# Expert slots from both ends: half of each expert's blocks gathered without the routing of the last four sequences

## The chip, the cores and the metric

The kernel runs on one core of a Trainium2 chip. The metric is the device time of one execution in microseconds (us); the median of several executions is compared. Of the core's engines, PE is TensorE's matmuls (PEld its weight loads), DVE is VectorE, ACT ScalarE, POOL GpSimd and SP SyncE. Every engine works through its own instructions in order. SP and POOL issue the DMAs of this case; POOL issues the indirect ones, which gather or scatter rows by an index held in SBUF.

## The reference

Thirty-two sequences of 256 tokens with 256 features each (8192 tokens) go through two layers. The first layer is a modulated linear map, a gated attention, an adapter, and a block of self-attention and a mixture of experts. The second is a linear attention with adapters and a feed-forward network whose two matrices are products of ten butterfly stages each. What matters here is the mixture of experts, cut short:

```python
C = 0.25 * T                                    # 2048 slots for each of 8 experts
logits = x @ wr;  probs = softmax(logits)
top1 = argmax(probs);  top2 = argmax(logits without top1)
loc1 = cumsum(m1, axis=0) - 1                   # m1, m2: one-hot of the choices
loc2 = cumsum(m2, axis=0) - 1 + m1.sum(0)       # second choices behind all first ones
m1 = m1 * (loc1 < C);  m2 = m2 * (loc2 < C)     # what doesn't fit is dropped
t1, t2 = probs of the kept choices, divided by their sum
# each expert: relu(x w1 + b1) w2 + b2 over its slots; y times t1 or t2 is added to the token
```

Which slot of its expert a token gets makes no difference to the result, as long as the same choices are dropped.

## The kernel before, in words

The program has two phases. The first makes the first layer up to the routing logits `L_all`, sequence after sequence. The second has the experts, the making of the butterfly matrices, and the second layer ("answers"). Between them stands a branch on a value read from memory (L1440), by which the first phase can be computed again in another form; it isn't taken here. No instruction of the second phase starts before it.

Within a phase, parts of the program are Python generators, which a planner (`side_by_side`, L100) runs side by side when the program is built. `yield PE, 0.5` gives the engine and the cost of the next piece, `yield "join", part` waits for another part, `get` and `back` take and return a tile of a ring, and `Turns` limit how many parts are in a section. The planner simulates the engines with these costs, takes what can start first (by order in the list at L2465 where several can), and so fixes the order of instructions on each engine. Rings: "mm" (the 8 PSUM banks), "sh" (small work tiles in SBUF, among them gathered rows `xg`, products `ysb` and butterfly products `bft`), and "big" (weights, hidden activations, butterfly weights `bfw`).

Routing goes by 64 token tiles of 128 tokens (`NT`). The last 8 (`LATE`), which are the last four sequences, are routed in the second phase, since their logits come last; the 56 before ("early") while the first phase still runs (`routed_early`, L664). The steps are the same for both:

- `choices_of` (L526) finds both choices on DVE (L548 to L556).
- `places_of` (L559) counts choices by tile and expert on PE (`cnt`, L569) and adds counts of tiles before and a triangular product (`loc`, L582 and L584) to the place of every choice in its expert (`nths`). All first choices of an expert are numbered through and so are the second choices.
- `tokens_of` (L597) turns places into slots and inverts the map: one-hot products on PE (`tps`, L626; one-hots from DVE and ACT) give the token in each slot. First choices get slots from the front of an expert (0, 1, ...), second choices from the back (2047, 2046, ...).

In `routing` (L1503), the second phase's part, the two halves are added (`both`, L1514), `late` tells which slots hold a second choice, and `tok` (L1520) is the table of tokens by slot. `ends` (L1527) makes the masks `late` and `used` from the totals; `gates` (L1568) makes the weights, transposes them on PE (L1612) and writes them to `gbuf` in memory (L1618); `slots` makes index tables `grow` and `row`.

An expert has 2048 slots in 4 blocks of 512. `expert_block` (L1675) waits for `routed`, gathers the rows of a block in 4 gathers on POOL (L1686), transposes them on PE (L1700) into `ehT`, and multiplies by w1 (L1740) and w2 (L1757). `slot_gates` (L1627) gathers the weights of the block's slots (`gslot`, L1633), `ysb` is multiplied by them (L1772), and `add_to_tokens` (L1638) adds each 128 rows to the tokens by an indirect scatter (L1643), one at a time. `load_expert` (L1659) loads w1, w2 and b2 of an expert over SP; expert 1's loads and the butterfly's are held behind the first block's gathers by a small memset on POOL (`behind_gathers`, L1653). `butterflies` runs ten stages (L1799 to L1805, three sections each) on DVE; PE takes the first half's result at L1834.

Of the kernel before, what the change touches and what calls it, by code (L numbers as in the profile page):

```python
# [218 lines left out]
def network(ctx: ExitStack, tc: tile.TileContext, a: dict, out: bass.AP):  # L219
# [303 lines left out]
    cntb = cst.tile([P, 2, NSB], BF, name="cntb")  # L523
    early = cst.tile([P, 2, 2 * NHI], F, name="early")

# [34 lines left out]
    def places_of(a, b):  # L560

        W = b - a
        n0, n1 = a // SLAB, -(-b // SLAB)
        wide = [(min(b, (n + 1) * SLAB) - n * SLAB) * NE for n in range(n1)]
        cps = yield from get("mm", "cnt", [P, 2, NSB])
        yield PE, 0.07 * 2 * (n1 - n0)
        for k in range(2):
            for n in range(n0, n1):
                nc.tensor.matmul(  # L569
                    cps[: wide[n], k, n : n + 1], mbs[:, k, n * P : n * P + wide[n]], oneb, start=True, stop=True  # L570
                )
        for n in range(n0, n1):
            yield DVE, 0.15
            nc.vector.tensor_copy(cntb[: wide[n], :, n], cps[: wide[n], :, n])
        yield back("mm")
        step = 2 if 2 * W * NE <= 512 else 1
        for k0 in range(0, 2, step):
            shape = [P, step, W * NE]
            loc = yield from get("mm", "loc", shape)
            yield PE, (1 + n1) * step * (0.05 + W * 0.0065)  # L580
            for i in range(step):
                nc.tensor.matmul(loc[:, i, :], utb, mbs[:, k0 + i, a * NE : b * NE], start=True, stop=False)  # L582
                for n in range(n1):
                    nc.tensor.matmul(  # L584
                        loc[:, i, :], cntb[: wide[n], k0 + i, n : n + 1].to_broadcast([wide[n], P]),
                        before[: wide[n], n, a * NE : b * NE], start=False, stop=(n == n1 - 1),
                    )
            e3 = yield from get("sh", "e3", shape)
            yield DVE, 0.1 + step * W * 0.0095
            nc.vector.tensor_tensor(e3, loc, mbs[:, k0 : k0 + step, a * NE : b * NE], ALU.mult)  # L590
            yield back("mm")
            yield DVE, 0.1 + step * W * 0.0095
            nc.vector.tensor_reduce(
                nths[:, k0 : k0 + step, a:b], e3.rearrange("p k (t e) -> p k t e", e=NE), AX.X, ALU.add
            )
            yield back("sh")

    def tokens_of(a, b, wide, into):
# [10 lines left out]
        nc.vector.tensor_scalar(f[:, 0], nth, float(CAP), float(2 * NSL), ALU.is_gt, ALU.mult)  # L609
        for k, (op, at) in enumerate(((ALU.add, NE * CAP - 1), (ALU.subtract, (NE + 1) * CAP))):  # L610
            nc.vector.scalar_tensor_tensor(f[:, 1, k], firsts[:, k, a:b], -float(CAP), nth[:, k], ALU.mult, op)
            nc.vector.scalar_tensor_tensor(i[:, 0, k], f[:, 1, k], float(at), f[:, 0, k], ALU.add, ALU.add)
# [5 lines left out]
        yield back("sh")  # L618
        tps = yield from get("mm", "tps", [P, 2, 2 * NHI])
        into.append(tps)  # L620
        last = None

        def product(ol, oh, k, t, w):
            yield PE, 0.135 * w
            for i in range(w):
                nc.tensor.matmul(  # L626
                    tps[:, k, :], ol[:, i // 2, :, i % 2], oh[:, i // 2, :, :, i % 2].rearrange("p a h -> p (a h)"),
                    start=(t + i == 0), stop=(t + i == W - 1),
                )
            yield back("sh")  # L630
            yield back(wide)

        def by_place(ol, oh, o1, k, t, w, before):
            yield ACT, 0.15 + 0.125 * w
            nc.scalar.activation(oh[:, :, 1, :, :], o1, AF.Copy, scale=prow)
            yield back("sh")
            if before is not None:
                yield "join", before
            yield from product(ol, oh, k, t, w)
# [24 lines left out]
    def routed_early(sequences):  # L664
# [6 lines left out]
        yield from tokens_of(0, NT - LATE, "kk", got)  # L671
        yield DVE, 0.8
        nc.vector.tensor_copy(early, got[0])
        yield back("mm")

# [824 lines left out]
    used = column_h("used")  # L1500
    cc = wD.tile([P, 2, NE], F, name="cc")

    def routing():  # L1503
# [5 lines left out]
        yield from tokens_of(NT - LATE, NT, "big", got)  # L1509
        both = yield from get("sh", "both", [P, 2, 2, NHI])  # L1510
        to = wD.tile([P, 2, NHI], F, name="to")
        yield "join", counted
        yield DVE, 0.75
        nc.vector.tensor_add(both.rearrange("p k a h -> p k (a h)"), got[0], early)  # L1514
        yield back("mm")
        yield DVE2, 1.0
        nc.vector.tensor_tensor(to, both[:, 1], late.unsqueeze(1).to_broadcast([P, 2, NHI]), ALU.mult)
        nc.vector.tensor_add(to, to, both[:, 0])
        yield DVE, 0.3
        nc.vector.scalar_tensor_tensor(tok, to[:, 0], float(P), to[:, 1], ALU.mult, ALU.add)  # L1520
        yield back("sh")
        rest.append(Part(gates()))
# [4 lines left out]
    def ends():  # L1527

        ps = yield from get("mm", "mm", [P, 2, NE])
        yield PE, 0.5  # L1530
        for k in range(2):
            for n in range(NSB):
                w = min(SLAB, NT - n * SLAB) * NE
                nc.tensor.matmul(
                    ps[:, k, :], cntb[:w, k, n : n + 1].to_broadcast([w, P]), e8b[:w],
                    start=(n == 0), stop=(n == NSB - 1),
                )
        yield DVE, 0.15
        nc.vector.tensor_copy(cc, ps)
        yield back("mm")  # L1540
        from_ = wD.tile([P, NE], F, name="from_")
        E3 = [P, NE, CAP // P]
        yield DVE, 1.0
        nc.vector.tensor_scalar(from_, cc[:, 1, :], -1.0, float(CAP), ALU.mult, ALU.add)
        for o, v in ((late, cc[:, 0, :]), (used, from_)):
            nc.vector.tensor_tensor(
                o.rearrange("p (e h) -> p e h", e=NE), place.unsqueeze(1).to_broadcast(E3),
                v.unsqueeze(2).to_broadcast(E3), ALU.is_ge,
            )
        nc.vector.scalar_tensor_tensor(used, late, 0.0, used, ALU.is_equal, ALU.max)  # L1550

# [16 lines left out]
    def gates():  # L1568

        pr = yield from get("sh", "pr", W3)  # L1570
        e3 = yield from get("sh", "e3", W3)
        sm_, den = column("sm_"), column("den")
        yield DVE2, 0.7
        nc.vector.tensor_tensor(pr, L_all, bc(tops[:, 0, :]), ALU.subtract)
# [8 lines left out]
        for k in range(2):  # L1583
            m = mbs[:, k, :].rearrange("p (t e) -> p t e", e=NE)
            s_ = nths[:, k, :]
            if k == 1:

                s_ = column("s1")
                yield DVE2, 0.7
                nc.vector.tensor_tensor(e3, m, cc[:, 0, :].unsqueeze(1).to_broadcast(W3), ALU.mult)  # L1590
                yield DVE, 0.9
                nc.vector.tensor_reduce(s_, e3, AX.X, ALU.add)
                nc.vector.tensor_add(s_, s_, nths[:, k, :])
            g = column(f"g{k}")
# [31 lines left out]

    def slot_gates(j0):  # L1627
        for p in rest:
            yield "join", p
# [20 lines left out]

    gathered, turned_first = Part(_ for _ in ()), Part(_ for _ in ())

# [6 lines left out]
    def load_expert(e, w):  # L1659
# [6 lines left out]
        yield SP, 0.1  # L1666
        nc.sync.dma_start(w["w1"], a["w1"][e].rearrange("(c p) f -> p c f", p=P))
        yield SP, 0.1
        nc.sync.dma_start(w["w2"], a["w2"][e].rearrange("(f p) d -> p f d", p=P))
        yield SP, 0.1  # L1670
        nc.sync.dma_start(w["b2"], a["b2"][e : e + 1, :].to_broadcast([P, D]))
        yield DMA, 10.5
        yield None, 2.0

    def expert_block(e, blk, w, loaded, routed):  # L1675
        yield lanes_b
        yield "join", routed
        s0 = e * CAP + blk * CBLK
# [5 lines left out]
        for t in range(QT_):  # L1684
            j = s0 // P + t
            nc.gpsimd.indirect_dma_start(  # L1686
                xg[t], None, h2buf[:, :], bass.IndirectOffsetOnAxis(ap=tok[:, j : j + 1], axis=0)
            )
# [24 lines left out]
        yield weights  # L1713
        yield "join", loaded
        yield hid_turn
# [14 lines left out]
        for q0 in range(0, QT_, wide):  # L1730
# [17 lines left out]
            for p in rs:  # L1748
                yield "join", p
            each = 1 if last else 2  # L1750
            for t0 in range(q0, q0 + wide, each):
                n = min(each, QT_ - t0)
# [710 lines left out]
    with tc.manual_schedule():  # L2463
        side_by_side(
            [routed, loads[0], blocks[0], loads[1], matrices, *blocks[1:], weights_part, *loads[2:], table_part, *first_parts, square_part, norm_part, rows_part]  # L2465
            + [Part(answer_out(b, first_parts[-10] if b < 2 else norm_part, [norm_part])) for b in range(B)],
# [127 lines left out]
```

## Time and profile before

| | us |
|---|---|
| median of 3 runs | 3633.08 |
| lowest, highest | 3620.55, 3637.11 |
| profiled execution | 3623.08 |
| its span in the profile | 3621.3 |
| PE busy | 3432.9 (95%) |
| DVE busy | 2221.3 (61%) |
| ACT busy | 1795.8 (50%) |
| POOL busy | 1901.0 (52%) |

The mean granted clock of PE was 0.98. The span is from the first to the last instruction that the profile shows; the profiled execution's own time is 1.8 us longer. Times in the profile are counted from the span's start, so the border between the phases lies near 1580. A line of a timeline has start, duration, engine, line, operation, output and inputs with their shapes, the number of instructions in the group, and in brackets how long the engine was idle before it and what released it. Groups of DMA issues on POOL show the time that POOL spends on issuing one, not that of the transfer.

### The profile page before, as it was taken

To read this page: it belongs to the slowest core of one execution; us is meant where nothing else is said; L and a number is where in the kernel's file an instruction comes from. 1 tells how busy PE (TensorE), PEld (TensorE's weight loads), DVE (VectorE), ACT (ScalarE), POOL (GpSimd) and SP (SyncE) were. 2 spreads that over 40 slices of the span, in tenths; PEclk is the share of its full clock that TensorE was granted. 3 is DMA by queue.
4 is the path that set the end of the run, shared out by engine and by line. 5 is a ranking of instruction groups with operands and counts; after the bars stand their busy time and mean duration, and the time that the engine had idled before them with its cause. 6 is when DMAs were issued, how large, how long until landed. Compare 5 with 4: busy or idle time off the path is not lost. (4 is left out here: it accounts for less than half of the span.)

```text
span 3621.3 us, 55140 instructions
## 1 busy us (share of the span) xinstructions
PE 3432.9 (95%) x21397; PEld 2515.5 (69%) x21397; DVE 2221.3 (61%) x3664; ACT 1795.8 (50%) x2765; POOL 1901.0 (52%) x1533
## 2 busy tenths in 40 slices
PE   6798999999999999959999999999989999999999
PEld 5465566666666666636666666667978888888888
DVE  7988889888788983647665620101355565555553
ACT  2677787887787877722222222223224433343342
POOL 3655756565565564226555565553124565655553
PEclk9999999999999999979999999999989999999999
DMA  3344344433443442143334433332532233323321
GB/s 88 66 93 102 87 99 104 110 95 92 109 98 89 99 104 63 53 145 88 89 98 105 111 66 54 57 64 52 172 113 65 96 96 96 110 89 122 99 94 44
DMA packets 192240, 332.68 MB, mean 92 GB/s; under 512 B 55041, under 2 KB 116673, under 8 KB 181730
## 3 DMA queue, kind: packets, MB, share of 16 engines
q0 software_dynamic: 56768, 163.68, 20.3%
q1 hardware_dynamic: 135058, 164.86, 14.5%
q8 instruction: 171, 2.80, 0.3%
q14 instruction: 99, 0.81, 0.1%
q10 hardware_dynamic: 144, 0.52, 0.0%
HBM read 204.03 MB, written 52.58 MB: 71 GB/s over the span
## 5 line engine op out<-in xcount | busy, mean ns | idle before, releaser
L1090 ACT ACTIVATE pt<-sc 128x2048 f32<-128x2048 f32 x256 | 481.8, 1882 | 120.3 <-PE sc L1081 113.6
L1727 ACT ACTIVATE hid<-bh,cols 128x512 f32<-128x512 f32 (+1 forms) x261 | 175.9, 674 | 606.5 <-PE bh L1740 606.5
L1757 PE MATMUL by<-w,hid 128*128 128x256 f32 x2048 | 452.2, 379 | 0.0
L1740 PE MATMUL bh<-ehT,w 128*128 128x512 f32 (+1 forms) x1056 | 450.6, 581 | 0.1
L1757 PEld LDWEIGHTS by<-w,hid 128*128 128x128 f32 x2048 | 387.1, 190 | 65.6 <-issue 15.8
L267 POOL TENSOR_TENSOR n<-n,negh 128x32 f32<-128x32 f32 x64 | 363.6, 5681 | 5.3
L1643 POOL DMA_INDIRECT rrows<-ysb,row x128 | 220.6, 1724 | 255.5 <-DMA rrows<-ysb,row 141.2
L1740 PEld LDWEIGHTS bh<-ehT,w 128*128 128x128 f32 x1056 | 200.5, 191 | 216.4 <-issue 207.0
L1763 DVE TENSOR_TENSOR ysb<-by,b 128x512 f32<-128x512 f32 (+1 forms) x66 | 44.5, 674 | 483.9 <-PE by L1757 464.8
L1081 PE MATMUL sc<-qT,kT 32*128 32x256 f32 x4096 | 297.7, 405 | 14.3 <-ACT pt L1090 12.5
L1063 PE MATMUL av<-pt,vaug 128*32 128x256 f32 x4096 | 275.8, 387 | 7.1 <-ACT pt L1090 6.3
L893 DVE TENSOR_TENSOR hprod<-hex,kk 128x2048 f32<-128x2048 f32 x120 | 275.9, 2320 | 0.0
L1081 PEld LDWEIGHTS sc<-qT,kT 32*128 32x128 f32 x4096 | 187.4, 186 | 102.4 <-issue 51.9
L2419 PE MATMUL dh<-zT,w_eff 128*128 128x256 f32 x1024 | 236.3, 379 | 0.7 <-ACT zT L2391 0.7
L2433 PE MATMUL do<-w_con,gT 128*128 128x256 f32 x1024 | 230.5, 379 | 0.0
L2433 PEld LDWEIGHTS do<-w_con,gT 128*128 128x128 f32 x1024 | 192.5, 190 | 25.1
L1686 POOL DMA_INDIRECT xg<-h2buf,tok x128 | 138.4, 1082 | 134.8 <-issue 32.8
L261 POOL TENSOR_SCALAR rstd<-mv 128x2 f32<-128x2 f32 x160 | 53.1, 332 | 292.4 <-DVE mv L367 268.9
L2419 PEld LDWEIGHTS dh<-zT,w_eff 128*128 128x128 f32 x1024 | 188.9, 190 | 23.8 <-ACT zT L2391 1.1
L1063 PEld LDWEIGHTS av<-pt,vaug 128*32 128x32 f32 x4096 | 107.2, 109 | 135.3 <-issue 67.2
L261 POOL TENSOR_SCALAR n<-n 128x32 f32<-128x32 f32 x64 | 53.0, 828 | 237.7 <-DVE n L939 236.6
L1633 POOL DMA_INDIRECT gslot<-gbuf,grow x128 | 149.8, 1170 | 45.5 <-issue 37.8
(627 smaller groups left out, 7204.0 us busy)
## 6 DMA issues: line engine op xcount, KB each, us to landing
hprod<-hprod POOLq DMA_DIRECT2D x60, 1024.0 KB, 8.0
oT<-rden SPq DMA_DIRECT2D x64, 256.0 KB
w<-in_w SPq DMA_DIRECT2D x16, 1024.0 KB
x<-rrows SPq DMA_DIRECT2D x64, 256.0 KB
bfw<-in_upw SPq DMA_DIRECT2D x10, 1024.0 KB
bfw<-in_dnw SPq DMA_DIRECT2D x10, 1024.0 KB
xT<-in_xT SPq DMA_DIRECT2D x32, 256.0 KB
avT<-avT SPq DMA_DIRECT2D x256, 32.0 KB
```

The source lines that it names most:

```text
L267: nc.gpsimd.tensor_tensor(o, o, negh[:p].to_broadcast([p, n]), ALU.pow)
L893: nc.vector.tensor_tensor(pr.rearrange("p j (h d) -> p j h d", d=DH), weights(t, j0, 8)[:, 0].unsqueeze(3).to_broadcast([P, 8, H, DH]), wi ...
L1063: nc.tensor.matmul(av[32 * i : 32 * i + 32, c % 2, :], va[:, kc, HO * (4 * c + i) : HO * (4 * c + i) + 32], pt[:, i, kc, :], start=(kc == ...
L1081: nc.tensor.matmul(sc[:, i, kc, :], kT[r, m, kc * P : (kc + 1) * P], qT[r, e, m, :], start=True, stop=nm is None,)
L1090: nc.scalar.activation(pt, sc, AF.Exp, scale=1.0 / math.sqrt(DH))
L1633: nc.gpsimd.indirect_dma_start(gslot[:, j : j + 1], None, gbuf[:, :], bass.IndirectOffsetOnAxis(ap=grow[:, j : j + 1], axis=0))
L1643: nc.gpsimd.indirect_dma_start(rrows[:, :], bass.IndirectOffsetOnAxis(ap=row[:, j0 + t : j0 + t + 1], axis=0), y[:, t, :], None, compute_o ...
L1727: nc.scalar.activation(o, ps, AF.Relu, bias=bcol)
L1740: nc.tensor.matmul(ps, w["w1"][:, c, f * P : (f + 1) * P], hT[c][:, c0 : c0 + wide * P], start=(c == 0), stop=(c == 1))
L1757: nc.tensor.matmul(ps[:, t, :], hid[f // 4][:, f % 4, (t0 + t) * P : (t0 + t + 1) * P], w["w2"][:, f, :], start=(f == 0), stop=(f == 7),)
L2419: nc.tensor.matmul(ps[:, g, :], w_eff[:, c, f * P : (f + 1) * P], zT[:, c, :], start=(c == 0), stop=(c == 1))
L2433: nc.tensor.matmul(ps[:, t, :], gT[:, f, t * P : (t + 1) * P], w_con[:, f, :], start=(f == 0), stop=(f == 7))
```

## The change

Slots of an expert are now filled from the front by the early tokens (first choices, then second ones) and from the back by the late tokens. An expert's early tokens alone then fix what lies in the first slots, up to where early choices end. `early` is turned into a token table `etok` in the first phase. Blocks 0 and 1 of each expert (`ahead`, the slots below 1024) gather by `etok` and don't wait for `routed`; blocks 2 and 3 gather by `tok` as before.

Counts of the late tiles go to a table of their own (`lcnt`). For the second choices `places_of` adds the total of the first choices of the same group of tiles, which takes a matmul more per slab. `tokens_of` sums both choices in one PSUM tile. `ends` makes four borders of each expert (where early first choices end, where all early ones end, where late ones start, and where their second choices start) by 10 matmuls and some twenty small DVE operations instead of 8 and 4, and the masks from these. `gates` computes both choices' places with added totals. The wait for `routed` moves from the block to `slot_gates`, a pause of 6 us is put into the late one-hot products for the planner, expert 0's w2 and b2 are held behind the first gathers (its block waits for w1 first and for w2 before the second product), and the list of parts begins with expert 0's load and its first two blocks, ahead of `routed`.

```diff
     def places_of(a, b):
+        counts = cntb if a == 0 else lcnt
...
             for i in range(step):
                 nc.tensor.matmul(loc[:, i, :], utb, mbs[:, k0 + i, a * NE : b * NE], start=True, stop=False)
-                for n in range(n1):
+                for n in range(n0, n1):
+                    w = wide[n]
+                    if k0 + i == 1:
+                        nc.tensor.matmul(
+                            loc[:, i, :].rearrange("p (t e) -> p t e", e=NE), counts[:w, 0, n : n + 1].to_broadcast([w, P]),
+                            e8b[:w].unsqueeze(1).to_broadcast([w, W, NE]), start=False, stop=False,
+                        )
...
     def tokens_of(a, b, wide, into):
-        for k, (op, at) in enumerate(((ALU.add, NE * CAP - 1), (ALU.subtract, (NE + 1) * CAP))):
+        op, at = (ALU.add, NE * CAP - 1) if a == 0 else (ALU.subtract, (NE + 1) * CAP)
+        for k in range(2):
...
-        tps = yield from get("mm", "tps", [P, 2, 2 * NHI])
+        tps = yield from get("mm", "tps", [P, 2, NHI])
...
+            if a > 0:
+                yield None, 6.0
...
     def routed_early(sequences):
         nc.vector.tensor_copy(early, got[0])
+        nc.vector.scalar_tensor_tensor(etok, early[:, 0], float(P), early[:, 1], ALU.mult, ALU.add)
...
     def routing():
-        nc.vector.tensor_add(both.rearrange("p k a h -> p k (a h)"), got[0], early)
+        nc.vector.tensor_tensor(to, got[0], of_late.unsqueeze(1).to_broadcast([P, 2, NHI]), ALU.mult)
...
-        nc.vector.tensor_tensor(to, both[:, 1], late.unsqueeze(1).to_broadcast([P, 2, NHI]), ALU.mult)
-        nc.vector.tensor_add(to, to, both[:, 0])
+        nc.vector.tensor_tensor(early, early, of_early.unsqueeze(1).to_broadcast([P, 2, NHI]), ALU.mult)
+        nc.vector.tensor_add(to, to, early)
...
     def ends():
+        for c, (a, b) in enumerate(((0, border), (border, NT))):
...
+        nc.vector.tensor_add(early_end, first_end, kept[:, 0])
+        nc.vector.tensor_add(second_end, first_end, room)
+        nc.vector.tensor_add(late_start, early_end, room)
+        nc.vector.tensor_tensor(late_start, late_start, kept[:, 1], ALU.subtract)
+        for i in range(4):
...
+        nc.vector.tensor_copy(of_late, g3)
+        nc.vector.tensor_scalar(of_early, g2, -1.0, 1.0, ALU.mult, ALU.add)
+        nc.vector.tensor_add(used, of_early, of_late)
...
     def slot_gates(j0):
+        yield "join", routed
...
     def load_expert(e, w):
+        if e == 0:
+            yield DMA, 3.0
+            yield None, 2.0
+            yield first_half
+            yield from behind_gathers(w["w2"][:, 0, 0:1])
...
     def expert_block(e, blk, w, loaded, routed):
         yield lanes_b
-        yield "join", routed
+        ahead = blk < (CAP - LATE * P) // CBLK
+        if not ahead:
+            yield "join", routed
...
-                xg[t], None, h2buf[:, :], bass.IndirectOffsetOnAxis(ap=tok[:, j : j + 1], axis=0)
+                xg[t], None, h2buf[:, :], bass.IndirectOffsetOnAxis(ap=(etok if ahead else tok)[:, j : j + 1], axis=0)
...
-        yield "join", loaded
+        yield "join", first_half if e == 0 else loaded
...
-            [routed, loads[0], blocks[0], loads[1], matrices, *blocks[1:], weights_part, *loads[2:], table_part, *first_parts, square_part, norm_part, rows_part]
+            [loads[0], blocks[0], blocks[1], routed, loads[1], matrices, *blocks[2:], weights_part, *loads[2:], table_part, *first_parts, square_part, norm_part, rows_part]
```

## The prediction

> **What bounds the kernel now.** I read the slices first, because they show where TensorE (PE) is not full.
>
> ```profile
> ## 2 busy tenths in 40 slices
> PE   6798999999999999959999999999989999999999
> ...
> DVE  7988889888788983647665620101355565555553
> ...
> POOL 3655756565565564226555565553124565655553
> ```
>
> PE is the bound nearly everywhere. Slice 17 (a digit is 90.5 us; 1539 to 1630) is the one hole in the middle: the border between the two phases, which is where the change works. The table by stretches (columns: PE, PEld, DVE, ACT, POOL busy with counts, granted clock, DMA share, GB/s) cuts it finer.
>
> ```profile
> 1540.00:1580.00 40.00, 19.05 (x170) 12.46 (x162) 8.56 (x23) 10.86 (x12) 4.34 (x6) 0.75 0.14 43
> 1580.00:1606.00 26.00, 8.16 (x45) 5.08 (x46) 20.83 (x62) 4.28 (x5) 7.14 (x9) 0.57 0.42 136
> 1606.00:1900.00 294.00, 293.96 (x1079) 196.07 (x1078) 192.77 (x250) 72.28 (x106) 170.03 (x125) 1.00 0.40 110
> ```
>
> So PE idles 21 us in the tail of the first phase and 18 us before the first expert matmul, and then has not one wait for 294 us. In the timeline of the border:
>
> ```profile
> 1577.96 0.17 ACT L1379 COPY L_all<-mm 128x16 f32<-128x16 f32 x1 [1.54 <-PE mm L1374]
> ...
> 1581.29 0.22 DVE L548 TENSOR_REDUCE tops<-L_all 128x8 f32<-128x64 f32 x1 [6.88 <-ACTq L1440]
> ...
> 1589.92 3.57 PE L626 MATMUL tps<-oh,ol 128*128 128x256 bf16 x16 [4.01 <-ACT oh L635]
> ...
> 1595.17 0.29 DVE L1520 SCALAR_TENSOR_TENSOR tok<-to 128x128 int32<-128x128 f32 x1
> ...
> 1597.18 1.16 POOL L1686 DMA_INDIRECT xg<-h2buf,tok  x1 [23.55 <-DVE rf L1562]
> ...
> 1605.46 8.24 PE L1740 MATMUL bh<-ehT,w 128*128 128x512 f32 x16
> ```
>
> The second phase starts at about 1581.3; the routing of the last sequences ends with `tok` at 1595.46, POOL's first gather starts at 1597.18 after 23.55 us of waiting, and the first expert matmul 8.3 us after that. Everything behind is PE without a gap; the waits of PE after 1606 sum to some 29 us, none before about 2500. A microsecond removed ahead of 1605.46 counts in full only if PE still finds no wait behind it. That second half is what I worry about, because the supply behind the gathers is not idle:
>
> ```profile
> 1624.26 1.46 POOL L1633 DMA_INDIRECT gslot<-gbuf,grow  x1 [6.79 <-DMA gbuf<-g12T]
> ...
> 1631.71 2.09 POOL L1643 DMA_INDIRECT rrows<-ysb,row  x1 [0.45 <-DVE ysb L1772]
> ...
> 1641.58 3.40 POOL L1633 DMA_INDIRECT gslot<-gbuf,grow  x1 [0.30 <-issue]
> ```
>
> ```profile
> 1658.20 1.09 DVE L1799 TENSOR_TENSOR bft<-w_eff,bfw 128x512 f32<-128x512 f32 x1 [9.57 <-DMA rrows<-ysb,row]
> ...
> 1874.85 0.68 DVE L1805 TENSOR_TENSOR bfb<-bfb,bft 1x512 f32<-1x512 f32 x1
> ...
> 1884.50 1.94 PE L1834 MATMUL mm<-ones,bfb 1*128 1x1 f32 x16
> ```
>
> POOL carries all gathers and scatters one after the other. DVE (VectorE) has the butterflies, whose work tiles share a ring with `ysb`, so that a late scatter holds a stage up (9.57 us at 1658.20). Their first half ends at 1875.5 and PE takes its result at 1884.5: 9 us of margin.
>
> **The change, part by part**, against the profiled execution (3623.08 us); the median of the runs shown is 10.0 us above it, which I add at the end. Times below are on the clock of before.
>
> *A. Tail of the first phase.* Counts and slots of the first 28 sequences are done by PE in the same place, with an added matmul per slab for second choices; a one-hot product is as long as before (16 passes, 1.98 us at 1531.03). In the changed order the first scores of the last sequence stand behind all of these products, where before 8 of them (1.08 us at 1540.20) came after the scores. The tail behind those scores is a chain of latencies, so what is put ahead of it counts: two groups of 1.08 and the added matmuls, +3 us (0, if the scores are late anyway, to +6).
>
> *B. The hole.* Blocks 0 and 1 of expert 0 gather by `etok`, which is ready in the first phase. POOL's first gather can go when the second phase starts, at about 1581.7 instead of 1597.18. From first gather to first expert matmul it was 8.3 us, which gives 1590; but PE has the counts (`cnt`, 1583.23 and 1584.77) and `loc` in its order between the transposes, w1 comes at the same time as four gathers, and ACT makes both `ehT`. I take 1592: -13.5 us (-11 to -15.5, the end where nothing is added). The half-speed start stays, it only comes earlier.
>
> *C. Routing under the experts.* 16 one-hot passes (1.98 us at full clock) and 10 count matmuls (8 took 0.38) are no longer in the hole but between expert matmuls: +2.5.
>
> *D. The rest's routing is now late.* A block is 32 matmuls by w1 (L1740, 13.8 us; the second 16 of block 0 took 7.03) and two product groups by w2 (L1757, 7.07 each at 1620.96 and 1630.89). PE's new order is: the first of these of block 0 (1.7 us more at half clock), one product group, half of the one-hot products, block 1's 32 matmuls by w1, the other one-hot products, one product group, then the transposes of blocks 2 and 3. PE is there at 1592 + 1.7 + 13.8 + 7.1 + 13.8 + 7.1 + about 3.5 of small matmuls = 1639. The last one-hot product ends at about 1632, and DVE makes `tok` by 1634.5. That is 39 us later than before, and POOL's eight gathers for blocks 2 and 3, 1.25 us each, end at 1646 and land 3 us after. DVE needs for the gates 11.3 us from `tok` to the last `g` in before (1595.46 to 1606.8) and two products more now: until about 1648.7, and the gates' transpose (L1612) stands in PE's queue right behind the gathered rows. PE, which is through at 1639 plus 2 us of transposes, waits to 1648.7: +6.5 us (+4 to +14). Queued behind it are all later matmuls. Nobody waited there before.
>
> *E. POOL's backlog.* From the gates' transpose to the first `gslot` gather it was 10.7 us (1613.54 to 1624.26): the first comes at about 1655 or later (the write of the gates stands behind a butterfly load on SP's queue) instead of 1624.26, and the first scatter eight gathers of 1.45 later, about 1666 instead of 1631.7. In POOL's new order follow two scatters (5.1 us apart), 4 gathers, 1 scatter, 4 gathers, 3 scatters, and then expert 1's rows: 1666 + 10 + 6 + 5 + 6 + 15 = 1708, plus 1 for landing of the first. PE asks for them one product group before expert 0 ends, at about 1704: +4.5 us (0 to +10).
>
> By the Trainium skill (page "SBUF — State Buffer", section "SBUF: two separate sides"), a DVE instruction that takes the port it shares with GpSimd keeps GpSimd from writing the descriptors of its own DMAs, and such a DMA goes from some 620 to 3100 ns. The 3.40 us `gslot` gather above, beside a butterfly product, looks like it, but the mean of 48 such gathers up to 1900 is 1.26 us, nearly all of them with butterflies running, so the trace has it as the exception. By the rule alone the first eight `gslot` gathers, now beside a stage, would cost an estimated 13 us more and E would be +17.
>
> *F. The butterflies.* In DVE's order the first stage (three times 5.5 us) now stands ahead of `tok` (this is why `tok` isn't earlier) and the gates between it and the second stage, which begins at 1649 instead of 1641.05. In it before, a product waited for the fourth scatter to land (issued 1654.50). By the order in E the fourth scatter goes out at about 1693, so up to 39 us later. The stage that waited then ends between 8 and 39 us later, and with it the chain: between 1884 and 1914, and somewhat later if more stages find their ring full. PE reaches L1834 at 1884.5 - 13.5 + 2.5 + 6.5 + 4.5, plus one more product group (7.1) and 12 more transposes (1.5) that now stand ahead of it: 1893. So the wait is 0 to some 25 us; the slips inside a stage are partly made up, since DVE spends 72 us of this stretch waiting for PE. I take the middle, +14. A wait that long also lowers the clock, as in the hole (first expert passes 0.85 us instead of 0.43): +1.5.
>
> Sum: 3 - 13.5 + 2.5 + 6.5 + 4.5 + 14 + 1.5 = +18.5. From 3623.1 that is 3641.6, on the scale of the median 3652. The extremes add to -11 and +45.
>
> **Rivals.** (1) *Not slower: the stalls are hidden.* If the planner's order leaves PE enough prepared work at D, POOL keeps its distance at E and the butterflies' chain catches up before L1834, only A, B and C are left: 3 - 13.5 + 2.5 = -8, some 3625. It decides if `gslot` for blocks 0 and 1 starts before 1645. For it: 294 us without a PE wait, a POOL 58% and a DVE 66% busy there. Against it: PE's order has the gates' transpose right ahead of the work that must not wait. (2) *Only D and E:* the chain of butterflies ends before PE gets to L1834: 3 - 13.5 + 2.5 + 6.5 + 4.5 = +3, some 3636. It decides if the fourth scatter is out by 1670. (3) *A larger pile:* the scatters' delay fills the ring of `ysb`, PE stops for PSUM too, or the chain ends at 1915 or later: D 10, E 8, F 25 with the clock: some +35, 3668 to 3680. (4) *The change doesn't do what it says*, the first gather still waits for something of the routing: no gain in B, and a loss near 20; it falls in (3).
>
> **How the numbers follow.** About 0.5% (18 us) is what can be told from no change here. Chances: the forecast case (3640 to 3664) 0.45, (1) 0.13, (2) 0.16, (3) with (4) 0.26. Faster than 3615 needs the whole of B's far end and nothing behind it, and a phase-one tail that gains: 0.09, out of (1). Slower than 3651 is half of the forecast case and (3): with a share of what I didn't see, 0.55. The rest, 0.36, lies between. The range from 3620 to 3680 leaves out one in ten at each side; the likeliest case alone is 3640 to 3664.
>
> **What would show it.** Right: the first `xg` gather at about 1582 after the tail's shift, the first L1740 some 13 us earlier against the phase's start, a PE wait at L1612 or at L1700 on `tok`'s rows of 5 us or more, the first L1643 scatter near 1666, a PE wait at L1834. Wrong: a first gather still behind the routing (B), PE at 100% in the 294 us after its first expert matmul (D, E, F), or a phase-one tail that moved by more than 6 us (A).

## The result, and the profile after

The changed kernel takes 3653.75 us (median of 6 runs, 3647.54 to 3656.47); the kernel before, with three more runs beside it, 3625.63 (6 runs). The ratio is 1.0071, with a 95% interval of 1.0058 to 1.0083: slower by 0.7%. The profiled execution of the changed kernel took 3653.26 us, its span is 3651.5, 30.2 us more than the span before.

The slices show where the hole went. The line below is PE's in the changed kernel:

```profile
PE   6798999999999999968989999999989999999999
```

A digit is 91.3 us now. Before, the one low digit in the middle was a 5 at slice 17 (counted from 0). Now there is a 6 there, and 8s at slice 18 (1643 to 1734) and slice 20 (1826 to 1917), where nines were. The stretches cut at the events (columns as before the change: PE, PEld, DVE, ACT, POOL, granted clock, DMA share, GB/s) show besides the hole itself (first line) three in which PE isn't full (the second, third and fifth line), all behind the first expert matmul at 1597.94:

```profile
1588.00:1598.00 10.00, 2.56 (x16) 1.95 (x16) 2.73 (x13) 0.88 (x2) 6.47 (x7) 0.50 0.53 178
1598.00:1653.50 55.50, 50.59 (x183) 30.30 (x180) 40.69 (x95) 18.72 (x26) 9.68 (x14) 0.93 0.49 169
1653.50:1719.00 65.50, 59.63 (x205) 39.44 (x205) 38.28 (x51) 13.54 (x21) 42.20 (x32) 0.94 0.30 76
1719.00:1905.00 186.00, 185.94 (x698) 127.72 (x696) 120.67 (x153) 41.33 (x60) 102.55 (x72) 1.00 0.37 99
1905.00:1930.00 25.00, 10.59 (x26) 6.58 (x27) 15.93 (x24) 3.25 (x5) 13.80 (x11) 0.59 0.26 58
```

Where the kernel before had 294 us of PE without a wait there are now losses at 1644 to 1653, at 1710 to 1718 and at 1905 to 1919. The timeline of PE names what each waits for (L1762, L1820, L1802 and L1897 are the changed file's lines for the transposes, the products by w2, by w1, and the bias of the up matrix):

```profile
1597.94 15.55 PE L1802 MATMUL bh<-ehT,w 128*128 128x512 f32 x32
...
1646.44 0.76 PE L1762 MATMUL mm<-ident,xg 128*128 128x128 f32 x5 [1.26 <-DMA xg<-h2buf,tok]
...
1653.50 15.08 PE L1820 MATMUL by<-w,hid 128*128 128x256 f32 x64
...
1712.95 0.30 PE L1762 MATMUL mm<-ident,xg 128*128 128x128 f32 x1 [2.65 <-DMA xg<-h2buf,etok]
...
1919.41 3.56 PE L1897 MATMUL mm<-ones,bfb 1*128 1x1 f32 x16 [14.47 <-DVE bfb L1864]
1922.91 18.62 PE L1802 MATMUL bh<-ehT,w 128*128 128x512 f32 x36
```

The last two lines also show the price of a long wait: 16 passes take 3.56 us instead of 1.94, and 36 passes by w1 take 18.62 where 36 took 15.61 elsewhere (1733.81), while the granted clock of the stretch is 0.59. POOL's timeline has the two moves of the change in it:

```profile
1589.70 1.16 POOL L1748 DMA_INDIRECT xg<-h2buf,etok  x1 [9.06 <-DVE e L554]
...
1639.35 1.15 POOL L1748 DMA_INDIRECT xg<-h2buf,tok  x1 [39.52 <-DVE tok L1539]
...
1656.69 1.21 POOL L1688 DMA_INDIRECT gslot<-gbuf,grow  x1 [7.06 <-DVE bft L1862]
...
1667.41 1.64 POOL L1698 DMA_INDIRECT rrows<-ysb,row  x1 [0.30 <-DVE bft L1862]
```

The first gather goes 1.5 us after the second phase's start (1588.20) instead of 15.9 after it; the gathers by `tok`, the weights of the slots and the first scatter are late. Counted from the first expert matmul, the first scatter comes after 69.5 us, where it was 26.2.

To compare executions I cut each profiled one at four events of its timeline: the counts of the early tiles on PE (first `cnt` matmul, in the first phase), the first instruction of the second phase, the first expert matmul, and the end of the last product by w2. Up to the counts PE has the same matmuls in the same order in all fourteen kernels, and yet those counts come between 1474.5 us (e8) and 1496.2 (e11) in their profiles; more on that at the end. The stretches behind them repeat better. A row's stretches are those of one profiled execution, its median is of 4 to 12 runs, and its ratio is to runs of the kernel before made beside it, whose medians were 3625.5 to 3627.5.

| kernel | counts to phase 2 | to first expert matmul | to last product | to the end | median, us | ratio to before (95%) |
|---|---|---|---|---|---|---|
| before | 97.6 | 24.2 | 912.5 | 1103.3 | 3625.6 | |
| changed | 103.8 | 9.7 | 951.3 | 1102.2 | 3653.8 | 1.0058 to 1.0083 |
| e1 routing first | 107.0 | 9.8 | 918.3 | 1105.0 | 3619.8 | 0.9976 to 1.0007 |
| e2 bias later | 104.9 | 9.8 | 955.4 | 1101.4 | 3659.0 | 1.0067 to 1.0100 |
| e3 old cost | 98.2 | 9.7 | 951.3 | 1100.5 | 3643.8 | 1.0037 to 1.0065 |
| e4 not ahead | 104.6 | 25.5 | 934.2 | 1101.8 | 3649.6 | 1.0055 to 1.0087 |
| e5 8 scatters left out | 103.9 | 9.8 | 942.6 | 1102.6 | 3642.5 | 1.0029 to 1.0058 |
| e6 own ring, seen by the planner | 106.3 | 9.8 | 950.6 | 1099.3 | 3647.8 | 1.0041 to 1.0083 |
| e7 routing first, old cost | 97.5 | 9.8 | 926.5 | 1102.5 | 3620.3 | 0.9969 to 0.9993 |
| e8 e7 with own ring | 97.8 | 9.8 | 926.8 | 1102.1 | 3622.1 | 0.9977 to 0.9998 |
| e9 routing first, old cost for early tiles | 97.4 | 9.8 | 918.4 | 1104.3 | 3609.0 | 0.9933 to 0.9960 |
| e10 gates not made | 106.1 | 9.8 | 952.3 | 1101.9 | 3651.1 | 1.0051 to 1.0089 |
| e11 own slots, same order | 104.2 | 9.8 | 934.4 | 1102.5 | 3647.1 | 1.0030 to 1.0065 |
| e12 e9 with own slots | 98.2 | 10.8 | 917.2 | 1101.7 | 3611.3 | 0.9940 to 0.9971 |

The change itself reads: 0.7 us later at the counts, 6.2 in the tail, 14.4 gained ahead of the first expert matmul, 38.8 lost behind it, 1.1 gained at the end: 30.2.

### The profile page after: what moved, and what is told of

It is laid out like the page before. It is cut to its first block, busy times and chain, and to the rows that moved or that the text cites. A ratio compares the mean times of both kernels' runs of the same rounds, so it can differ in the third digit from the quotient of the medians.

```text
span 3651.5 us, 55178 instructions
## 1 busy us (share of the span) xinstructions
PE 3444.4 (94%) x21398; PEld 2523.3 (69%) x21398; DVE 2227.5 (61%) x3686; ACT 1795.5 (49%) x2767; POOL 1887.3 (52%) x1534
## 5 line engine op out<-in xcount | busy, mean ns | idle before, releaser
L1820 PE MATMUL by<-w,hid 128*128 128x256 f32 x2048 | 454.7, 381 | 0.0
L1802 PE MATMUL bh<-ehT,w 128*128 128x512 f32 (+1 forms) x1056 | 453.5, 584 | 0.0
L1820 PEld LDWEIGHTS by<-w,hid 128*128 128x128 f32 x2048 | 389.5, 191 | 65.1 <-issue 14.1
L1802 PEld LDWEIGHTS bh<-ehT,w 128*128 128x128 f32 x1056 | 201.9, 192 | 218.1 <-issue 209.7
L1698 POOL DMA_INDIRECT rrows<-ysb,row x128 | 218.7, 1709 | 252.2 <-DMA rrows<-ysb,row 125.7
L817 DVE TENSOR_REDUCE hex<-hprod 128x64 f32<-128x1024 f32 (+1 forms) x192 | 166.6, 896 | 1.2
```

What stands on the lines that cost most here:

```text
L817: nc.vector.tensor_reduce(e[:, t, j0 : j0 + n, :] if exact else e[:, t, 8 : 8 + w // DH, j0 : j0 + n].rearrange("p h j -> p j h"), pr[:, t ...
L1698: nc.gpsimd.indirect_dma_start(rrows[:, :], bass.IndirectOffsetOnAxis(ap=row[:, j0 + t : j0 + t + 1], axis=0), y[:, t, :], None, compute_o ...
L1802: nc.tensor.matmul(ps, w["w1"][:, c, f * P : (f + 1) * P], hT[c][:, c0 : c0 + wide * P], start=(c == 0), stop=(c == 1))
L1820: nc.tensor.matmul(ps[:, t, :], hid[f // 4][:, f % 4, (t0 + t) * P : (t0 + t + 1) * P], w["w2"][:, f, :], start=(f == 0), stop=(f == 7),)
```

## The experiments

**e1: the order of the list.** One line differs from the changed kernel:

```diff
-            [loads[0], blocks[0], blocks[1], routed, loads[1], matrices, *blocks[2:], ...
+            [routed, loads[0], blocks[0], blocks[1], loads[1], matrices, *blocks[2:], ...
```

> The planner's list begins with the late routing, then expert 0's load and its first two blocks; nothing else of the changed kernel differs. Theory 1 (the late one-hot products stand behind two blocks of expert matmuls on PE; the waits at the rows of blocks 2 and 3, at expert 1's rows and at the up matrix's bias all follow from that): these three losses of 8.2, 8.5 and 19.1 us go, the earlier first matmul stays: 3653.8 - 35.8 = some 3618, no PE wait over 3 us between the first expert matmul and the answers. Theory 2 (the butterflies' chain is late of itself, by the gates' work on DVE): only 16.7 us go, some 3637, and the wait at the bias stays near 14 us. Theory 3 (the new slots cost work): no more than 3 us go, 3651 or more.

3619.8 us. PE's one-hot products now stand inside block 0's products by w1 (1612.65 and 1615.28, where the changed kernel had them at 1621.79 and 1636.43), and `tok` reaches POOL at 1618.20 instead of 1639.35:

```profile
1618.20 1.15 POOL L1748 DMA_INDIRECT xg<-h2buf,tok  x1 [16.40 <-DVE tok L1539]
```

The stretch to the last product falls from 951.3 to 918.3. The waits of PE from the counts on (waited for, total us, times, longest) have only one entry left that is new and behind the first expert matmul, the last line; the first line is the hole ahead of that matmul:

```profile
PE mm L1762 <- DMA xg<-h2buf,etok: 10.3, 2, 9.5
...
PE mm L1762 <- DVE ysb L1826: 1.9, 1, 1.9
```

So all three losses, taken together, come from the late routing's rank in the planner's list, theory 1; the new slots cost little here (918.3 against 912.5, with the wait of 1.9 in it).

**e2: the reader of the chain moved.** The matmuls of L1897 become a part of their own, which waits for block 12:

```diff
+    def up_bias(xb):
+        yield "join", blocks[12]
         ps = yield from get("mm", "mm", [P, 8])
...
-        ps = yield from get("mm", "mm", [P, 8])
...
-        yield back("big")
+        yield Part(up_bias(xb))
```

> The 16 passes that take the butterflies' first result (the bias of the up matrix) wait for block 12 to be done, three blocks later on PE; the rest is as in the changed kernel. Theory 1: the wait of 14.5 us and the lowered clock behind it (4.6 us) are a loss by the position in PE's queue alone: 3653.8 - 19.1 = 3635 (3631 to 3641). Theory 2 of this run (the ring of work tiles is short as well, and the wait moves on to the product groups): within 4 us of 3654.

Nothing is gained (955.4 to the last product, 3659.0 us, 1 us beyond what theory 2 allowed). PE doesn't wait at the bias, but 6.5 us in three pieces and 8.5 in one elsewhere:

```profile
1921.87 12.53 PE L1802 MATMUL bh<-ehT,w 128*128 128x512 f32 x22 [3.71 <-ACT ehT L1765]
1935.14 1.98 PE L1802 MATMUL bh<-ehT,w 128*128 128x512 f32 x4 [0.74 <-DVE ysb L1826]
1939.19 3.70 PE L1802 MATMUL bh<-ehT,w 128*128 128x512 f32 x8 [2.06 <-ACT ehT L1765]
...
2094.29 9.11 PE L1820 MATMUL by<-w,hid 128*128 128x256 f32 x32 [8.51 <-DVE ysb L1826]
```

Theory 1 of this run falls: moving the reader doesn't remove the loss. DVE itself stood still before it, 14.73 us at 1916.42 (13.73 at 1903.07 in the changed kernel), at a butterfly product that waits for a scatter.

**e3: the planner's cost in the first phase.**

```diff
-            yield PE, (1 + n1 - n0) * step * 1.5 * (0.05 + W * 0.0065)
+            yield PE, (1 + n1) * step * (0.05 + W * 0.0065)
```

> The planner's cost of the place matmuls (the yield ahead of L590) is set back to the expression of before; the instructions stay. By the list of instructions PE's order in the first phase is then that of before with the added matmuls only. Theory 1 (6.9 us of the first phase's tail are 5.4 of a new wait of an output projection and its slow clock, and 1.5 of the added matmuls): the second phase starts 5.4 us earlier, at about 1582.8, and the time is 3648. Theory 2 (as predicted, the tail is set by the one-hot products ahead of the last scores): the start moves by 1 to 2 us. All waits behind the first expert matmul stay as they are.

From the counts to the second phase 98.2 us instead of 103.8, and 951.3 again behind the first expert matmul: theory 1. The median falls by 10 us, of which the stretches behind the counts explain 7.3 (2159.7 against 2167.0). The largest single piece is a wait of an output projection of the first phase, with 1.4 us for running at a low clock behind it. The first line is the changed kernel's, the second e3's:

```profile
1498.24 3.36 PE L317 MATMUL mm<-w_wo,oT 128*128 128x256 f32 x8 [3.46 <-DVE oT L1157]
...
1491.97 1.99 PE L317 MATMUL mm<-w_wo,oT 128*128 128x256 f32 x8 [1.42 <-DVE oT L1157]
```

So the wait gets 2.0 us shorter and doesn't go. Another 1.2 us are gained at the last projection, which waits 11.80 us instead of 13.04. The old cost also puts the one-hot products back in their old places, so what these cost by themselves isn't told apart.

**e4: the gain given up.** New slots, but all blocks gather by `tok`, in the list's order of before:

```diff
-        ahead = blk < (CAP - LATE * P) // CBLK
+        ahead = False
...
-            [loads[0], blocks[0], blocks[1], routed, loads[1], matrices, *blocks[2:], ...
+            [routed, loads[0], blocks[0], loads[1], matrices, *blocks[1:], ...
```

> New slots as in the changed kernel, but every block gathers by tok and waits for the routing, and the list of parts is that of before. Theory 1: the first phase's 6.9 us stay, the first gather is 3 to 4 us later after the start of the phase than in the kernel before (21 small operations instead of 4, and two masked products), and there are no PE waits behind it: 3625.6 + 6.9 + 3.5 = 3636, faster than the changed kernel though its early gathers are given up. Theory 3 (the new slots cost the time): 3653.8 + 14 = 3668.

A miss: 3649.6, not 3636. The first gather comes 1.2 us later after the phase's start than before (17.1 against 15.9), less than expected, but 934.2 to the last product is 21.6 us more than before, and the waits are none of the three:

```profile
2094.86 9.70 PE L1820 MATMUL by<-w,hid 128*128 128x256 f32 x32 [6.50 <-DVE ysb L1826]
...
2182.63 10.16 PE L1802 MATMUL bh<-ehT,w 128*128 128x512 f32 x16 [4.42 <-ACT ehT L1765]
```

With a third one of 2.7 us these waits sum to 13.6 of the 21.6; slow passes behind the two shown add 2.6 and 3.1 (9.70 us for 32 passes that take 7.07 elsewhere, 10.16 for 16 that take 7.03). So this region has hardly any slack: an order that the planner made with slightly other costs and times meets waits of this kind hundreds of us later. Why just there was not tried.

**e5: fewer scatters.** Guarded by `if j0 + t >= 8`, eight scatters go; the order of all else stays.

> Left out of the computation: the scatters of the first 8 slot tiles of expert 0 (blocks 0 and 1), so their results are not added to the tokens. All other instructions stay in the changed kernel's order on every engine. The run with the bias later showed the wait at the bias to move on when its place is moved, so the question is what is late. Theory 1 (scatters: POOL's backlog keeps slots of the work ring, DVE stands at a butterfly product until they land, PE then waits for DVE): 8 scatters at 4.7 to 6 us apart are some 40 us off POOL's queue ahead of expert 1's rows; the wait there (8.5 us with the clock) and at the bias (19.1) go, 3653.8 - 27.6 = 3626 (to 3634), DVE's waits for scatters fall from 54 us to under 20. Theory 2 (as predicted in part: the gates' work on DVE between the first two stages makes the chain late): only expert 1's rows gain, 3645, and the bias waits 10 us or more.

By the numbers theory 2: the time is 3642.5, only expert 1's rows gain, and DVE's waits for scatters fall to 34.8 us, not under 20. To the last product it is 942.6, 8.7 less: the wait at expert 1's rows (8.5 with its clock) is gone, which shows it to be POOL's backlog. The wait at the bias is still there:

```profile
1911.93 3.57 PE L1898 MATMUL mm<-ones,bfb 1*128 1x1 f32 x16 [15.62 <-DVE bfb L1865]
```

The scatters of the first blocks are not what DVE waits for 250 us later. Theory 2's reason, the gates, is the next run's question.

**e10: the gates not made.** The instructions of `gates` ahead of the transpose are left out, and two memsets write the gates.

> Left out of the computation: the making of the gates (22 instructions of DVE and one of ACT); all gates are 0.25. Everything else stays in the changed kernel's order on every engine. Theory A (my step F: the gates on DVE between the butterflies' first two stages make the chain late): DVE has some 11 us more before the second stage, the wait at the bias falls from 14.5 us to 4 or less; with D's 5 us the time is some 3654 - 19 = 3635. Theory B (the chain is late by scatters that stand behind waiting gathers in POOL's order, wherever it was before): D gains 3 to 5 us, the wait at the bias stays at 12 us or more: 3649.

Nothing is gained at all: 952.3. The bias waits 15.58 us (1917.15), so my step's reason, the gates' work between the butterflies' stages, falls. D's 3 to 5 us aren't gained either. The rows of blocks 2 and 3 still land one by one, which is what PE waits for there:

```profile
1643.03 0.77 PE L1758 MATMUL mm<-ident,xg 128*128 128x128 f32 x5 [0.91 <-DMA xg<-h2buf,tok]
...
1645.46 0.33 PE L1758 MATMUL mm<-ident,xg 128*128 128x128 f32 x1 [0.96 <-DMA xg<-h2buf,tok]
1646.75 0.48 PE L1758 MATMUL mm<-ident,xg 128*128 128x128 f32 x1 [0.96 <-DMA xg<-h2buf,tok]
```

**e6 and e11: the shared slots.** Both give the butterflies' products three slots of their own. In e6 the planner sees them and writes another order; in e11 it goes on counting them in the shared ring, so the order of every engine stays.

```diff
+    bfts = pb.enter_context(tc.tile_pool(name="bfts", bufs=3))
...
-            r = yield from get("sh", "bft", [p, FF // 2])
+            yield rings["sh"][2]
+            r = bfts.tile([p, FF // 2], F, name="bft", tag="bft")
```

> The butterflies' products get a ring of 3 slots of their own; otherwise the changed kernel (the planner, which sees the slots, then moves some product groups). Theory 1 (scatters hold up DVE through the shared ring): DVE waits for no scatter at a butterfly product, the wait at the bias goes, 3653.8 - 19.1 = 3635; those at blocks 2 and 3 and at expert 1's rows stay. Rival (the backlog itself is the limit, and the product groups' tiles run out next): 3648 or more, with waits of PE for the tiles of products.

> The butterflies' products take their tiles from 3 slots of their own, while the planner still counts them in the shared ring, so that the order of every engine is that of the changed kernel. In the run with an own ring that the planner saw, the wait at the bias went and others came in a changed order. Theory 1 (the wait for scatters through the shared slots is the cause of the loss): DVE waits for no scatter at a product, the wait at the bias goes and none of its size comes: from the first expert matmul to the last product 951 - 19 = 932, the time 3635. Theory 2 (PE waits for scatters anyway, now through the tiles of products): 945 or more, 3648 or more.

By its time (3647.8) e6 is where the rival had it, not theory 1: DVE's 54 us of waits for scatters and the wait at the bias are gone, but in the new order waits of 4.17 us (for `ysb`, 1979), 2.04 and 3.47 us (for expert rows, 2020 and 2138) come instead, and the stretch is 950.6. In e11 every engine keeps the changed kernel's order, and the stretch is 934.4, 16.9 us less and nearly the 932 of theory 1. The waits of DVE between 1600 and 1960, first of the kernel before, then of the changed kernel:

```profile
DVE bft L1799 <- DMA rrows<-ysb,row: 19.6, 3, 9.6
...
DVE bft L1862 <- DMA rrows<-ysb,row: 54.1, 8, 13.7
DVE ysb L1826 <- PE by L1820: 51.8, 8, 13.2
```

and of e11, where the first of these is no longer in the list:

```profile
DVE ysb L1827 <- PE by L1821: 76.8, 12, 18.8
DVE ysb L1827 <- issue: 11.1, 1, 11.1
```

PE's wait at the bias is gone too. The two other losses remain (at expert 1's rows PE waits 3.08 and 4.47 us). So the stretch shows theory 1, but the time doesn't: the median is 3647.1 of four runs (3641.4 to 3648.9), where theory 1 had 3635 and theory 2 3648 or more. In the profiled execution (3648.87) the difference lies in the first phase, whose counts come at 1496.2 instead of 1484.4. The other three have no profile; the mean granted clock of all four, 0.975 to 0.977, is no higher than the changed kernel's (0.974 to 0.977). The slots as such don't make the first phase late: e12 has them too, and its counts come at 1475.4.

**e7, e8: both orders mended, first try.** Routing first and the old cost (e7), and with e6's ring (e8).

> Routing first in the list and the old planner's cost of the place matmuls together. Theory: the two act in different phases and add up: from the counts to the second phase 98 us (107 in the run with routing first), and no more than 6 us of losses behind the first expert matmul: 3619.8 - 8.8 = 3611, 0.4% under the kernel before. Rival (the two phases' orders aren't independent, or the tail takes the gain back): 3617 or more.

> Routing first, old cost and the own ring of the butterflies. If the shared ring is what is left of the losses behind the first expert matmul (5.8 us in the run with routing first, about 3 of them the routing's own matmuls): 3611 - 3 = 3608. Rival (nothing is left there that the ring could give): 3611, the same as without it.

Both miss by 9 to 14 us. The tail is gained (97.5), but to the last product it is 926.5, since the old cost also went to the late tiles and the second phase got another order, with a wait of 8.50 us for `ehT` at 2197.86. The own ring gives nothing there.

**e9 and e12: the better versions.** The old cost for the early tiles alone, so that the second phase has e1's order; e12 adds e11's slots.

```diff
-            yield PE, (1 + n1 - n0) * step * 1.5 * (0.05 + W * 0.0065)
+            yield PE, ((1 + n1) if a == 0 else 1.5 * (1 + n1 - n0)) * step * (0.05 + W * 0.0065)
...
-            [loads[0], blocks[0], blocks[1], routed, loads[1], matrices, *blocks[2:], ...
+            [routed, loads[0], blocks[0], blocks[1], loads[1], matrices, *blocks[2:], ...
```

> Routing first in the list, and the old cost of the place matmuls for the early tiles alone; so the first phase has the order of the run with the old cost, and the second phase, on every engine, that of the run with routing first. In the run with both edits the old cost had also been given to the late tiles, which gave the second phase another order. Theory: from the counts to the second phase 98 us, to the first expert matmul 9.8, from there to the last product 918; 3619.8 - 9.2 = 3611 (3608 to 3614). Rival (the tail of the first phase gives nothing, or the loss of the run with both, 14 us behind the first expert matmul, isn't from the order): 3618 or more.

> The first of these runs (routing first, old cost for the early tiles) with the butterflies' products in slots of their own and the order kept. Theory: what is left behind the first expert matmul is the routing's own matmuls, 3 us, and some 3 us of waits of which the ring is part: 3611 - 2 = 3609. Rival: no difference from the run without it, 3611.

e9 takes 3609.0 us, ratio 0.9946 (0.9933 to 0.9960), and its stretches are the expected ones within a microsecond: it is faster than both kernels. Of the 18 us between the medians the stretches behind the counts explain 7.7 (2137.6 against 2129.9). The rest is in no profile: e9's profiled execution, 3623.85 us, is the slowest of its six, and its counts come 8.5 us later than those of the kernel before. e12 (3611.3) is not told apart from e9; 917.2 against 918.4 to the last product, where PE's longest wait is 1.2 us.

## Why the prediction was right, and where its steps were off

The forecast, 3652 us and slower, holds, and so does the mechanism: gain at the gathers, losses behind them. The nearness of the point has luck in it. The sum of the steps was +18.5 us on the profiled execution, and +30.2 were measured there. I had added 10.0 for the way from that execution to the median of three; with more runs that way is 2.5 us (3625.6 against 3623.1). The two errors, 11.7 and 7.5, cancel for the most part. Between the medians of six runs the change is 28.1 us. The extremes of the steps, with the clock's 1.5 at the upper end, add to -9 and +48, not to -11 and +45.

Step by step, forecast and measured:

- **A**, the tail: +3, measured +6.2 (103.8 against 97.6), just over the 6 us that the prediction had named as a sign of being wrong. Mis-sized, and its reason was at best a part: e3 gives 5.6 us back by one number in the planner's costs, and most of these are two waits of output projections (2.0 and 1.2 us longer than in e3) and 1.4 us of low clock, which the step didn't have. Of the added matmuls alone some 0.6 us are left (98.2 against 97.6).
- **B**, the hole: -13.5, measured -14.4 (24.2 to 9.7). Right.
- **C**, the routing among the products: +2.5, measured 3.0 (what is left of 38.8 when the three losses below are taken off).
- **D**, blocks 2 and 3: +6.5, measured 8.2: from 1644.24 to 1653.50, 9.3 us for transposes of about 2.3, and 1.1 us of low clock in the 64 passes behind. The size is right, the reason is not: I had let PE wait for the gates, but of its waits 4.4 us are for the rows by `tok`, landing 1.3 us apart, and only 0.5, the last one, for the gates; without the gates' work (e10) the rows still take 4.5.
- **E**, expert 1's rows: +4.5, measured 8.5 (7.98 us from 1709.70 to 1717.68 for 0.95 of transposes, and 1.4 of low clock). That it is POOL's backlog is shown by e5. On the clock of before (6.9 us back) PE was there at 1702.8 and the first row at 1706, where 1704 and 1709 had been assumed. What I had left out is that PE then waits for the other three rows too (0.83, 1.05 and 1.34 us), and the clock.
- **F**, the bias: +15.5 with the clock, measured 19.1 (14.5 of waiting, 1.6 and 3.0 of low clock). The place and the size were right, the reason only in part; and the size has luck in it, since the middle of the step's own 0 to 25 is 12.5, not 14, and a chain that ends between 1884 and 1914 for a PE at 1893 gives no more than 21. Not the gates between the stages (e10) nor the first scatters (e5), but slots that are shared by scatter sources and butterfly products (e11, by its profile) under an order written for other times (e1). That a late scatter holds up DVE through the shared slots was in the step. Moving the reader (e2) only moves the wait, which the step had not said: I read the 9 us of margin at L1834 as the thing that was lost.

POOL's queue in the changed kernel shows how a scatter can get so late: just ahead of those that DVE waits for in the end, it stands 23.13 us at a gather whose rows have no slot yet, and scatters follow behind it in order:

```profile
1842.16 1.04 POOL L1748 DMA_INDIRECT xg<-h2buf,tok  x1 [23.13 <-ACT ehT L1765]
```

That this gather is what made the scatter at 1903 late was not tried by itself.

Rival (1), a gain of 8 us with all stalls hidden, is what e9 came to (7.7 us from the counts on) when the routing had its place back. Rival (2) falls by the wait at the bias, rival (4) by the gather at 1589.70. What happened in D, E and F lies between the forecast and rival (3): 35.8 us, where the forecast had 26.5 and the rival 43; the chain ended at 1921, or 1914 on the clock of before.

By the section "SBUF: two separate sides" of the Trainium skill's page "SBUF — State Buffer" the prediction had an estimated 17 us for E. Here the first eight `gslot` gathers took 0.94 to 1.42 us each (1656.69 to 1666.17), the five from 1660.70 on while two-input instructions of the butterflies or of `ysb` ran on DVE, so no such price was paid. In the kernel before, two of the 48 gathers took 3.40 us (1641.58 and 1703.33), not one; what made them long is open. The page's own section "Who interferes with whom" fits better: it says that `tensor_tensor`, which these products are, has no 2-port mode, and it infers that it takes only the read side of the shared pair, while writing descriptors needs the write side.

## What to carry to other kernels

When a step of a chain is released early, ask where the rest of the chain now stands in each in-order queue: here the early gathers were worth 14 us, the rest's rank behind two blocks of matmuls cost 33 (951.3 against 918.3), and one place in a list decided. A ring shared by the sources of slow scatters and the temporaries of another engine ties queues together, and here the wait that showed at a reader went when the slots were parted (e11), not when the reader was moved (e2). A planner's cost is part of the kernel: a factor of 1.5 on the cost of the place matmuls cost 5.6 us (e3), and giving the better cost to the late tiles as well cost 8 (926.5 against 918.4).

## What the runs showed of the hardware that was not expected

All fourteen profiles have the same matmuls in the same order on PE up to the counts of the early tiles, and yet these come between 1474.5 us (e8) and 1496.2 (e11). Behind them the same order repeats within some 3 us (103.8 to 107.0 to the second phase where the first phase has the changed kernel's order, and 951.3 twice to the last product).

Most of the spread goes with PE's clock. In the traces' clock records that clock has two values here, full and half. Ahead of the counts it stood at half for 64.9 us in e3, 68.3 in e8 and 75.1 in the kernel before, and for 92.2, 92.2 and 102.4 in e9, e2 and e11, whose counts are the latest three (1492.2, 1493.3 and 1496.2). The first expert passes of the kernel before started 0.85 us apart at half clock and 0.43 at full, so the 34.1 us more at half clock in e11 than in e8 cost up to 17 of the 21.7 us between them; PE's idle time is also 7.1 us longer (114.5 against 107.4). Why the clock is low for longer in one execution than in another is open.
